# A new word order in the last triangle stage, y turned by VectorE for the last batch, and put-off pieces at fixed groups

## The chip, the cores and the metric

The kernel runs on one core of one Trainium2 chip. The metric is the device time of one execution in microseconds. A core has five engines that run their own instruction lists in order: TensorE (PE, with its weight loads PEld), VectorE (DVE), ScalarE (ACT), GpSimd (POOL) and SyncE (SP), which here issues nearly all DMAs. They wait for each other through semaphores.

## The reference, cut to what matters

Two layers on `x` of shape (4, 64, 64, 256), all in float32. The first is self-attention over the 4096 positions of each batch element, with a residual; the second takes its result, here called y, as a 64 x 64 grid of pairs and does "triangle" attention with 8 heads, then a layer norm, an MLP and another layer norm.

```python
# layer 0, per batch element, hw = 4096 positions
f, g, v = xt @ Wf + bf, xt @ Wg + bg, xt @ Wh + bh
beta = softmax(g @ f.T)                 # 4096 x 4096
y = x + (beta @ v) @ Wo + bo
# layer 1, N = 64, 8 heads of 32
q, k, v1, v2 = y @ Wq, y @ Wk, y @ Wv1, y @ Wv2
scores = einsum('bilhd,bljhd->biljh', q, k) / sqrt(32)
att = softmax(scores, axis=2)           # over l
out = einsum('biljh,bilhd,bljhd->bijhd', att, v1, v2)
h = layer_norm(y + out.reshape(...) @ Wo)
h = relu(h @ W1 + b1) @ W2 + b2 + h
return layer_norm(h)
```

## The kernel before, in words

The four batch elements ("batches" 0 to 3) go one after the other. Each has a first-layer stage and a triangle stage; what is left of batch 3 after its triangle runs in a closing loop. The program order is written out by hand: nothing reorders the instructions of an engine inside `run`. The last few lines of the kernel (1633 and on) stand outside of that, and the framework puts them where it finds room.

**First-layer stage (`layer0`).** It has 8 blocks of 512 queries, and each block has 8 groups g (k = g mod 8) of 512 keys. In a group TensorE makes scores (L552) and the weighted values (L579), ScalarE the exponentials e (L564), two buffers of them, and VectorE adds e into esum (L586; L584 in group 0). In group 7 VectorE folds esum and splits it into the tile `part` (L589 to L596). The finished block is worked off in the groups of the next block, by the list `parts`: in group 0 the denominator den on TensorE (L604), its reciprocal (L608) and two bounds (L618) on VectorE; in group 1 y itself (L631, L632) and its store; in groups 2 to 7 the projections q, k, v1, v2 (L646, L678), each copied by ScalarE to a staging tile of three (`st`) and stored by SyncE.

For b > 1 the groups also carry the *put-off pieces* of batch b - 2: 16 pieces of 256 tokens, each loaded back (`recall`), added to its residue and measured (`settle`, VectorE, L1073 to L1137), then `rooted` (ScalarE), `polished` (VectorE, L1175 to L1178), `scaled` (ScalarE, L1197) and `finish`ed (GpSimd, L1287 and L1288, and the store of the output at L1289). A piece starts in every third group: line 761 gives the groups after its start at which each step comes.

**Triangle stage (`next_layer1`, `step_words`).** 32 steps. A step has 8 products R0 to R7 of the turned weights and v2 (L1007); VectorE makes the first five of an even step and the first six of an odd one, GpSimd the others, into three and two buffers. Each product is accumulated by TensorE (A0 to A7, L1017) into two PSUM tiles, which ScalarE copies out (T0, T1, L1027). Further words: S sums (L932), W weights (L942), t turns them on TensorE (L959), c copies a part for GpSimd (L967), V the stationary operand (L986), sp/e scores of a later head pair and their exponentials (L905, L915). In between run the words of the pieces of the batch before: h heads (L1120 and the transposes that add y, L1125), sa statistics, fa affine, ht turning (L1220), hT and hU its copies (L1225), m and r the MLP's first half (L1253, L1262), z its second (L1273, L1279), so sums (L1151, L1155), rr roots, pp polish (on GpSimd, L1181 to L1192), fo affine and fi finish (GpSimd).

One *period* holds two steps (0 and 1 of each word's first digit) and one piece. `ORDER_LAST` lists the words of a period for batch 3. `A14/2` means accumulate product 4 of the odd step of the period two before; "/1" the period before; "/-1" the next. There are 12 periods with scores, and 16 pairs of steps in all. Batch 3's triangle finishes all pieces of batch 2 and begins pieces 0 and 1 of batch 3.

PSUM tiles come from three pools of two: scores and accumulators ("a"), pieces ("b": hp, htp, mp, zp), turned weights and others ("c"). A buffer is taken from those that were freed.

**Heads.** A piece's heads are Wo times the attention output plus y. y lies in memory with channels first, so TensorE turns it on its way into the sum, two transposes per half piece:

```python
            for cc in range(2):
                nc.tensor.matmul(
                    hp[:, n, ts(cc, P)], yc[:, cc, ts(n, P)], ident, start=False, stop=(cc == 1),
                    is_transpose=True,
                )
```

**Closing loop (`alone`).** 15 turns and an end, for the pieces of batch 3. In a turn TensorE does the heads of piece t+2, the turning of t+1, the second MLP half of t and the first of t+1; VectorE does the statistics of t+2 (`stats_a`), their polish, the residue of t+1 (L1244, L1245), the finish of t-1 (L1287, L1288), the addition and statistics of t (L1145, `stats_o`) and their polish, in this order; ScalarE makes the roots, affines, copies and `rectify`.

**Limits.** All sums and bounds of all batches are kept in `dens`; at the end two reductions over it (L1635, L1636) decide if a safe version must run (it does not).

Of the kernel before, what the change touches and what calls it, by code (L numbers as in the profile page):

```python
# [10 lines left out]
F32 = mybir.dt.float32  # L11
# [39 lines left out]
ORDER_LAST = """  # L51
    r0/1 A10/2 A11/2 m1/1 R14/2 R05/1 S1/1 R15/2 T10/2 sp/1 A14/2 A16/2 r1/1 e0/1 e1/1 A15/2 A05/1 T11/2 R04/1
    A04/1 z0/1 W1/1 R03/1 V1/1 fi/2 S0 z1/1 t1/1 so/1 R06/1 R00/1 c1/1 sa A03/1 R07/1 R02/1 A06/1 A02/1 A00/1
    rr/1 pp/1 W0 R01/1 A07/1 A01/1 fo/1 fa T01/1 R12/1 t0 T00/1 R17/1 h1/-1 sf/1 R13/1 h0/-1 f0/1 ht f1/1 R16/1
    hU A13/1 hT A12/1 A17/1 R11/1 c0 R10/1 m0 V0
""".split()
# [18 lines left out]
def attention_then_triangle_kernel(  # L75
# [130 lines left out]

    dens = ctile([P, NB, 256 + 16], "dens")

# [237 lines left out]
    class Late:  # L446
# [5 lines left out]
        def load(self, q):  # L452
            self.y = []
            for cc, tag in enumerate(("A", "yc")):
                t = work.tile([P, 512], F32, tag=tag, name="yb", bufs=1)
# [42 lines left out]
    def layer0(b, F, safe, rest, ahead):  # L498
# [7 lines left out]
        io["v2"] = dram.tile([N, C, N], F32, tag="v2", name="v2d")  # L506
        io["v1"] = dram.tile([T, C], F32, tag="v1", name="v1d")
        L = Layer1(b, io, safe)

# [104 lines left out]
        def bounds(qb):  # L614
            for j, (t, op) in enumerate(ends.pop(qb)):
                if not safe:
                    c0 = 256 + 2 * qb + j
                    nc.vector.tensor_reduce(dens[:, b, c0 : c0 + 1], t, AX.X, op)  # L618

# [6 lines left out]
        def output(qb):  # L626
            col = ts(qb, QB)
            o = oT.pop(qb)
            for cc in range(2):
                y_ps = pb("y")  # L630
                nc.tensor.matmul(y_ps, wo0_sb[:, 0, ts(cc, P)], o, start=True, stop=True)  # L631
                nc.vector.scalar_tensor_tensor(  # L632
                    y(qb, cc), y_ps, bo_sb[:, cc : cc + 1], yT[cc][:, col], ALU.add, ALU.add
                )
                nc.sync.dma_start(out=io["y"][ts(cc, P), col], in_=y(qb, cc))


# [90 lines left out]
        if late:  # L728
            parts[3] = [lambda qb: proj(qb, "k", 0)]
            parts[4] = [lambda qb: proj(qb, "v2", 0)]  # L730
            parts[5] = [proj1_half]
            parts[6] = [lambda qb: proj(qb, "q", 1)]
            parts[7] = [lambda qb: proj(qb, "k", 1)]
        last = NQB - 1
        for r in range(4):
            score(0, r)
        for g in range(8 * NQB):
# [112 lines left out]
    class Layer1:  # L850
        def __init__(self, b, io, safe):
            self.b, self.io, self.safe = b, io, safe

            self.aT = dram.tile([C, 2, N // 2, N], F32, tag="aT", name="aT")
            io["a"] = self.aT
            self.S, self.v2, self.qk, self.v1, self.att, self.ao = {}, {}, {}, {}, {}, {}
            self.R, self.begun, self.acc, self.rec, self.e = {}, {}, {}, {}, {}


# [61 lines left out]
        def sums(self, step):  # L921
# [8 lines left out]
            else:  # L930
                den = dens[:, self.b, ts(step, IG)]
            nc.vector.tensor_reduce(den, rows, AX.X, ALU.add)  # L932
# [109 lines left out]


    class Tokens:
        def __init__(self):
            self.ios = []
            self.A, self.htp = {}, {}
            self.h, self.hT, self.hT2, self.hid, self.z, self.zp, self.hps = {}, {}, {}, {}, {}, {}, {}
# [46 lines left out]
        def load(self, tt, far=False):  # L1095
# [4 lines left out]
            if far:  # L1100

                tag = ("v2", "S", "qk")[t % 3]
                both = big.tile([P, 2, 2, 256], F32, tag=tag, name="A", bufs=4 if tag == "v2" else 2)
                A, yc = both[:, 0].rearrange("p c (i j) -> p c i j", j=N), both[:, 1]
            else:
                A = work.tile([P, 2, 4, N], F32, tag="A", name="A", bufs=1)
                yc = work.tile([P, 2, 256], F32, tag="yc", name="yc", bufs=1)
# [3 lines left out]
            nc.sync.dma_start(out=yc, in_=io["y"][:, ts(t, 256)].rearrange("(c p) t -> p c t", p=P))  # L1111
            self.A[tt] = A, yc

        def heads(self, tt, n, psum=pb, new=None):
            if n == 0 if new is None else new:
                self.hps[tt] = psum("hp").rearrange("p (n c) -> p n c", n=2)
            hp = self.hps[tt]
            A, yc = self.A[tt]
            for cc in range(2):
                nc.tensor.matmul(  # L1120
                    hp[:, n, :], A[:, cc, ts(n, 2), :].rearrange("p i j -> p (i j)"), wo1_sb[:, cc, :],
                    start=(cc == 0), stop=False,
                )
            for cc in range(2):
                nc.tensor.matmul(  # L1125
                    hp[:, n, ts(cc, P)], yc[:, cc, ts(n, P)], ident, start=False, stop=(cc == 1),
                    is_transpose=True,
                )

# [8 lines left out]

        def stats_a(self, tt):
            self.stats(self.hps[tt], 0)  # L1140

# [292 lines left out]
    def first_layer1(L, ahead, F):  # L1434
# [56 lines left out]
    def next_layer1(b, L, rest, ahead, F):  # L1491
# [32 lines left out]
        def of_piece(word, q):  # L1524
# [9 lines left out]
            elif word == "sa" and first:  # L1534
                moments(q - 1)
                if own:
                    rest.stats(rest.hps[tt], 0)
# [53 lines left out]
        mps[1] = {}  # L1591
        for period in range(NP + 4):
            for word, late in words_of(ORDER_LAST if own else ORDER):
# [85 lines left out]
```

## Time and profile before

| | us |
|---|---|
| median of 3 runs | 3628.52 (3628.36 to 3633.21) |
| profiled execution | 3633.17 |
| its span, first to last instruction | 3631.40 |
| last triangle stage, from GpSimd's first product | from 3025.36 |
| first heads of the closing loop | 3472.68 |

| engine | busy us | share of the span |
|---|---|---|
| TensorE | 3522.3 | 97% |
| VectorE | 2823.5 | 78% |
| ScalarE | 1923.8 | 53% |
| GpSimd | 1779.2 | 49% |

How to read it: the span is the traced execution; the execution's own time is 1.8 us longer, and this execution was 4.65 us above the median. The ends of matmuls are modelled, so TensorE's busy time covers short gaps; the distance from one start to the next is what a word costs. A line with a bracket at its end tells how long the engine was idle before the instruction and what ended that. The mean granted TensorE clock of the profile is 0.994 of full speed.

### The profile page before, as it was taken

To read this page: it belongs to the slowest core of one execution; us is meant where nothing else is said; L and a number is where in the kernel's file an instruction comes from. 1 tells how busy PE (TensorE), PEld (TensorE's weight loads), DVE (VectorE), ACT (ScalarE), POOL (GpSimd) and SP (SyncE) were. 2 spreads that over 40 slices of the span, in tenths; PEclk is the share of its full clock that TensorE was granted. 3 is DMA by queue.
4 is the path that set the end of the run, shared out by engine and by line. 5 is a ranking of instruction groups with operands and counts; after the bars stand their busy time and mean duration, and the time that the engine had idled before them with its cause. 6 is when DMAs were issued, how large, how long until landed. Compare 5 with 4: busy or idle time off the path is not lost.

```text
span 3631.4 us, 58644 instructions
## 1 busy us (share of the span) xinstructions
PE 3522.3 (97%) x22282; PEld 1895.3 (52%) x22282; DVE 2823.5 (78%) x2558; ACT 1923.8 (53%) x4221; POOL 1779.2 (49%) x904
## 2 busy tenths in 40 slices
PE   9999999988999999999999999999899999999998
PEld 6555444434555555554455555554455555555477
DVE  4777499996555569999777549999877756999976
ACT  3444455544444366665444446666444436777655
POOL 5000099995000068889211018889611106999920
PEclk9999999999999999999999999999999999999999
DMA  9544555455111354425423254343622235441221
GB/s 174 135 131 127 136 151 137 122 134 136 47 52 52 82 145 108 101 68 107 110 91 95 67 146 109 89 104 76 132 87 95 80 93 134 92 96 46 68 68 55
DMA packets 492594, 370.15 MB, mean 102 GB/s; under 512 B 303184, under 2 KB 434000, under 8 KB 483472
## 3 DMA queue, kind: packets, MB, share of 16 engines
q1 hardware_dynamic: 443264, 339.36, 34.8%
q0 software_dynamic: 36160, 19.94, 5.3%
q10 hardware_dynamic: 12880, 7.01, 0.7%
q8 instruction: 178, 2.92, 0.4%
q14 instruction: 112, 0.92, 0.1%
HBM read 205.73 MB, written 160.43 MB: 101 GB/s over the span
## 4 chain that ended last, share of the span: by engine, by line
PE 67%; POOL 8%; DVE 6%; issue 4%; ACT 1%; DMA 1%; SPq 0%; ACTq 0%; POOLq 0%; DVEq 0%
PE o L579 16%; PE acc L1017 16%; POOL Rp L1007 7%; PE proj L646 6%; PE mp L1253 5%; PE zp L1273 5%; PE s L552 4%; PE sp L905 3%; PE hp L1120 3%; DVE R L1007 2%; PE v1p L678 2%; PE att L959 1%; PE y L631 1%; DVE rec L608 1%; PE htp L1220 1%
## 5 line engine op out<-in xcount | busy, mean ns | idle before, releaser
L1007 POOL TENSOR_TENSOR Rp<-attP,v 128x2048 f32<-128x2048 f32 x328 | 1491.4, 4579 | 409.7 <-ACT attP L967 367.0
L1007 DVE TENSOR_TENSOR R<-att,v 128x2048 f32<-128x2048 f32 x696 | 1546.1, 2279 | 68.6 <-PE acc L1017 49.9
L579 PE MATMUL o<-e,v 128*128 128x512 f32 x2048 | 1043.9, 593 | 0.0
L586 DVE TENSOR_TENSOR esum<-esum,e 128x2048 f32<-128x2048 f32 x224 | 518.8, 2316 | 398.4 <-ACT e L564 395.9
L564 ACT ACTIVATE e<-s 128x1024 f32<-128x1024 f32 x512 | 522.3, 1023 | 529.2 <-PE s L552 438.7
L552 PE MATMUL s<-gT,fT 128*128 128x512 f32 x1024 | 786.7, 770 | 8.7 <-ACT e L564 4.7
L1017 PE MATMUL acc<-R,wsel 128*32 128x512 f32 x5568 | 702.8, 599 | 26.5 <-DVE R L1007 19.6
L579 PEld LDWEIGHTS o<-e,v 128*128 128x128 f32 x2048 | 388.2, 190 | 276.8 <-issue 234.0
L1027 ACT COPY ao<-acc 128x1024 f32<-128x1024 f32 x256 | 256.4, 1013 | 290.4 <-PE acc L1017 205.8
L1017 PE MATMUL acc<-Rp,wsel 128*32 128x512 f32 x2624 | 344.3, 596 | 25.6 <-POOL Rp L1007 23.2
L1017 PEld LDWEIGHTS acc<-R,wsel 128*32 128x32 f32 x5568 | 155.5, 109 | 393.7 <-issue 273.9
L552 PEld LDWEIGHTS s<-gT,fT 128*128 128x128 f32 x1024 | 194.5, 190 | 244.7 <-issue 230.8
L1287 POOL TENSOR_TENSOR hz<-hz,log_bc 128x512 f32<-128x512 f32 x32 | 47.1, 1471 | 542.8 <-ACT hz L1197 474.4
L1181 POOL TENSOR_SCALAR nt<-mv 128x2 f32<-128x2 f32 (+1 forms) x49 | 9.4, 192 | 565.2 <-DVE mv L1137 560.1
L942 ACT ACTIVATE es<-S,rd 128x64 f32<-128x64 f32 x1024 | 258.3, 338 | 15.0 <-DVE rd L934 13.1
L1253 PE MATMUL mp<-hT,w 128*128 128x256 f32 x1024 | 244.4, 384 | 1.7 <-ACT hT L1225 1.7
L1273 PE MATMUL zp<-w,hid 128*128 128x256 f32 x1024 | 239.4, 384 | 0.8 <-ACT hid L1262 0.8
L1253 PEld LDWEIGHTS mp<-hT,w 128*128 128x128 f32 x1024 | 186.5, 190 | 53.0 <-ACT attP L967 12.6
L1273 PEld LDWEIGHTS zp<-w,hid 128*128 128x128 f32 x1024 | 188.0, 190 | 47.8 <-issue 14.7
L608 DVE RECIPROCAL rec<-den 128x512 f32<-128x512 f32 x32 | 107.4, 3357 | 109.7 <-PE den L604 104.4
L1017 PEld LDWEIGHTS acc<-Rp,wsel 128*32 128x32 f32 x2624 | 80.7, 110 | 214.1 <-issue 144.9
L915 ACT ACTIVATE S<-sp 128x512 f32<-128x512 f32 x128 | 131.6, 1094 | 78.0 <-PE sp L905 78.0
(192 smaller groups left out, 3688.4 us busy)
## 6 DMA issues: line engine op xcount, KB each, us to landing
v<-v2d SPq DMA_DIRECT2D x44, 512.0 KB
v1c<-v1d SPq DMA_DIRECT2D x128, 128.0 KB
aT<-ao SPq DMA_DIRECT2D x1024, 16.0 KB
A<-aT SPq DMA_DIRECT2D x256, 64.0 KB
hz<-raw SPq DMA_DIRECT2D x32, 512.0 KB
y<-yT SPq DMA_DIRECT2D x56, 256.0 KB
q<-st SPq DMA_DIRECT2D x56, 256.0 KB
k<-st SPq DMA_DIRECT2D x52, 256.0 KB
```

Of the source, the lines that this page charges most:

```text
L552: nc.tensor.matmul(s_ps[r // 2][:, r % 2, :], fT[tt][:, ts(r * 4 + n, P)], gT[qb // 4][:, ts(qb % 4, QB)], start=True, stop=not safe,)
L564: nc.scalar.activation(e[g][:, 2 * j : 2 * j + 2, :], s_ps[j], AF.Exp)
L579: nc.tensor.matmul(o_ps[qb], F.v[tt][:, r * 4 + n, :], es[:, r, :], start=(k == 0 and r == 0), stop=(k == 7 and r == 3),)
L586: nc.vector.tensor_tensor(esum[qb], esum[qb], es, ALU.add)
L608: nc.vector.reciprocal(rec, den)
L646: nc.tensor.matmul(ps, w[:, cc, rows], y(qb, cc), start=(cc == 0), stop=(cc == 1))
L942: nc.scalar.mul(e[:, i, :], rows[:, i, :], rec[:, i : i + 1])
L1007: eng.tensor_tensor(R, src.unsqueeze(1).to_broadcast([P, D, N]), v2[h], ALU.mult)
L1017: nc.tensor.matmul(acc[32 * c : 32 * c + 32, n % 2, :], w[:, n, c, 16 * h : 16 * h + 32], R[:, ts(c, 8), :].rearrange("p d j -> p (d j)"), ...
L1027: nc.scalar.copy(self.ao[step][:, ts(np, 2)].rearrange("p k d j -> p k (d j)"), self.acc[step][np])
L1253: nc.tensor.matmul(self.mp[:, fc % 2, :], w1_sb[:, cc, ts(fc, P)], self.hT[tt][:, cc, :], start=(cc == 0), stop=(cc == 1),)
L1273: nc.tensor.matmul(zp[:, n, :], self.hid[tt][:, fc, ts(n, P)], w2_sb[:, fc, :], start=(fc == 0), stop=(fc == 3 and tt not in self.hT2),)
```

## The change

Five edits:

1. `ORDER_LAST` has its words in another order, and some of them with another period. The rule that moved two words of the first period (A05, A04) is dropped.
2. For batch 3 (`turned_ahead`), y is also kept with tokens first, in a new buffer `yt`. VectorE turns it block by block in 32 x 32 squares (`turn_y`): blocks 0 to 6 in group 5 of the next block, with the tile in the buffer that `part` uses ("hid"); the last after its bounds, with its stores put off to the start of period 1 of the triangle (`L.owed`). Each block goes out in four stores in runs of 256 bytes.
3. The heads of batch 3 have no transposes. Before the statistics VectorE adds the loaded rows of `yt` to the heads in PSUM (`add_y`).
4. The put-off pieces have fixed places in a block: three pieces in blocks 0 and 1, two in 2 to 6, none in 7, with the settles in groups 2, 3 and (third piece) 5.
5. `dens` holds one batch; each batch's limits are reduced in group 1 of the next batch's first layer, the last batch's at the end.

```diff
-    r0/1 A10/2 A11/2 m1/1 R14/2 R05/1 S1/1 R15/2 T10/2 sp/1 A14/2 A16/2 r1/1 e0/1 e1/1 A15/2 A05/1 T11/2 R04/1
-    A04/1 z0/1 W1/1 R03/1 V1/1 fi/2 S0 z1/1 t1/1 so/1 R06/1 R00/1 c1/1 sa A03/1 R07/1 R02/1 A06/1 A02/1 A00/1
-    rr/1 pp/1 W0 R01/1 A07/1 A01/1 fo/1 fa T01/1 R12/1 t0 T00/1 R17/1 h1/-1 sf/1 R13/1 h0/-1 f0/1 ht f1/1 R16/1
-    hU A13/1 hT A12/1 A17/1 R11/1 c0 R10/1 m0 V0
+    A07/2 sf/2 T01/2 f0/2 R16/2 sp/1 f1/2 A10/2 R17/2 fa/1 fo/2 A12/2 R15/2 S1/1 ht/1 h1 e1/1 fi/2 h0 hU/1 hT/1
+    e0/1 t0/1 R13/2 m0/1 r0/1 A13/2 R14/2 A14/2 R11/2 A15/2 c0/1 A16/2 V0/1 W1/1 A17/2 A11/2 R00/1 V1/1 R01/1
+    m1/1 t1/1 R05/1 S0 T11/2 T10/2 r1/1 A00/1 W0 R03/1 A01/1 R06/1 A05/1 c1/1 R02/1 z1/1 R04/1 z0/1 A02/1 so/1
+    A03/1 R07/1 sa rr/1 R10/1 R12/1 T00/1 A06/1 pp/1 A04/1
...
-    dens = ctile([P, NB, 256 + 16], "dens")
+    dens = ctile([P, 256 + 16], "dens")
+    lims = ctile([P, 2, NB], "lims")
+    def limits(b):
+        for j, op in enumerate((ALU.min, ALU.max)):
+            nc.vector.tensor_reduce(lims[:, j, b : b + 1], dens, AX.X, op)
...
+        def turn_y(qb, **where):
+            t = work.tile([P, 16, 2, 32], F32, name="yr", **where)
+            for cc in range(2):
+                rows = y(qb, cc).rearrange("p (k t) -> p k t", t=32)
+                for k in range(4):
+                    nc.vector.transpose(t[:, ts(k, 4), cc, :], rows[:, ts(k, 4), :])
+            def kept():
+                for r in range(4):
+                    nc.sync.dma_start(
+                        out=io["yt"][ts(qb, QB), ts(r, 64)].rearrange("(k t) c -> t k c", t=32),
+                        in_=t[ts(r, 32)].rearrange("t k h c -> t k (h c)"),
+                    )
+            return kept
...
+        if turned_ahead(b):
+            parts[5].append(lambda qb: turn_y(qb, tag="hid", bufs=1)())
...
-                for do, late in ((rest.finish, 7), (rest.scaled, 6), (rest.polished, 5), (rest.rooted, 4), (rest.settle, 3), (rest.recall, 0)):
-                    if (g - late) % 3 == 0 and 0 <= g - late < 3 * NP:
-                        do(NP * (b - 2) + (g - late) // 3)
+                first = 3 * qb if qb < 2 else 2 + 2 * qb
+                for t in range(3 if qb < 2 else 2 if qb < last else 0):
+                    for do, at in (
+                        (rest.recall, t), (rest.settle, 2 + t + t // 2), (rest.rooted, 3 + t + t // 2),
+                        (rest.polished, 4 + t + t // 2), (rest.scaled, 5 + t + t // 2), (rest.finish, 7),
+                    ):
+                        if k == min(at, 7):
+                            do(NP * (b - 2) + first + t)
+            if g == 1 and b > 0 and not safe:
+                limits(b - 1)
...
         bounds(last)
+        if turned_ahead(b):
+            L.owed = turn_y(last, tag="k8")
...
+            src = io["yt"][ts(t, 256)] if turned_ahead(b) else io["y"][:, ts(t, 256)]
+            nc.sync.dma_start(out=yt, in_=src.rearrange("(n p) c -> p n c", p=P))
...
-                    start=(cc == 0), stop=False,
-                )
-            for cc in range(2):
-                nc.tensor.matmul(
-                    hp[:, n, ts(cc, P)], yc[:, cc, ts(n, P)], ident, start=False, stop=(cc == 1),
-                    is_transpose=True,
-                )
+                    start=(cc == 0), stop=(cc == 1 and turned_ahead(tt // NP)),
+                )
+            if not turned_ahead(tt // NP):
+                for cc in range(2):
+                    nc.tensor.matmul(
+                        hp[:, n, ts(cc, P)], self.yt[tt][:, cc, ts(n, P)], ident, start=False, stop=(cc == 1),
+                        is_transpose=True,
+                    )
+
+        def add_y(self, tt):
+            hp, yt = self.hps[tt], self.yt.pop(tt)
+            if not turned_ahead(tt // NP):
+                return
+            for n in range(2):
+                own = hp[:, n, :].rearrange("p (h r c) -> p h r c", h=2, r=4)
+                nc.vector.tensor_tensor(own, own, yt[:, n, :].rearrange("p (r h c) -> p h r c", h=2, r=4), ALU.add)
...
         def stats_a(self, tt):
+            self.add_y(tt)
             self.stats(self.hps[tt], 0)
...
         for period in range(NP + 4):
+            if period == 1:
+                L.owed()
             for word, late in words_of(ORDER_LAST if own else ORDER):
                 i = period - late
-                if own and i == 0 and word in ("A05", "A04"):
-                    for m in (4, 5) if word == "A04" else ():
-                        step_word("A", 0, m)
-                elif word[0] in "RATSWVtc":
+                if word[0] in "RATSWVtc":
...
-    flat = dens.rearrange("p b n -> p (b n)")
-    nc.vector.tensor_reduce(lim[:, 0:1], flat, AX.X, ALU.min)
-    nc.vector.tensor_reduce(lim[:, 1:2], flat, AX.X, ALU.max)
+    limits(NB - 1)
+    nc.vector.tensor_reduce(lim[:, 0:1], lims[:, 0], AX.X, ALU.min)
+    nc.vector.tensor_reduce(lim[:, 1:2], lims[:, 1], AX.X, ALU.max)
```

More of the change, by code (lines that the diff above doesn't have):

```diff
@@ L453, in load @@
             self.y = []
-            for cc, tag in enumerate(("A", "yc")):
-                t = work.tile([P, 512], F32, tag=tag, name="yb", bufs=1)
+            for cc, tag, bufs in ((0, "A", 1), (1, "yc", 1)):
+                t = work.tile([P, 512], F32, tag=tag, name="yb", bufs=bufs)
                 nc.sync.dma_start(out=t, in_=self.io["y"][ts(cc, P), ts(q, 512)])
@@ L507, in layer0 @@
         io["v1"] = dram.tile([T, C], F32, tag="v1", name="v1d")
+        io["yt"] = dram.tile([T, C], F32, tag="yt", name="yt")
         L = Layer1(b, io, safe)
@@ L617, in bounds @@
                     c0 = 256 + 2 * qb + j
-                    nc.vector.tensor_reduce(dens[:, b, c0 : c0 + 1], t, AX.X, op)
+                    nc.vector.tensor_reduce(dens[:, c0 : c0 + 1], t, AX.X, op)
         def y(qb, cc):
@@ L857, in __init__ @@
             self.R, self.begun, self.acc, self.rec, self.e = {}, {}, {}, {}, {}
+            self.owed = lambda: None
         def fetch_qk(self, pair, first=False):
@@ L930, in sums @@
             else:
-                den = dens[:, self.b, ts(step, IG)]
+                den = dens[:, ts(step, IG)]
             nc.vector.tensor_reduce(den, rows, AX.X, ALU.add)
@@ L1039, in store, with turned_ahead @@
                 )
+    def turned_ahead(b):
+        return b == NB - 1
     class Tokens:
@@ L1046, in __init__ @@
             self.ios = []
-            self.A, self.htp = {}, {}
+            self.A, self.yt, self.htp = {}, {}, {}
             self.h, self.hT, self.hT2, self.hid, self.z, self.zp, self.hps = {}, {}, {}, {}, {}, {}, {}
@@ L1103, in load @@
                 both = big.tile([P, 2, 2, 256], F32, tag=tag, name="A", bufs=4 if tag == "v2" else 2)
-                A, yc = both[:, 0].rearrange("p c (i j) -> p c i j", j=N), both[:, 1]
+                A, yt = both[:, 0].rearrange("p c (i j) -> p c i j", j=N), both[:, 1]
             else:
                 A = work.tile([P, 2, 4, N], F32, tag="A", name="A", bufs=1)
-                yc = work.tile([P, 2, 256], F32, tag="yc", name="yc", bufs=1)
+                yt = work.tile([P, 2, 256], F32, tag="yc", name="yt", bufs=1)
             for c in range(2):
@@ L1110, in load @@
                     nc.sync.dma_start(out=A[:, c, o : 4 : 2, :], in_=io["a"][ts(c, P), o, ts(t, 2), :])
-            nc.sync.dma_start(out=yc, in_=io["y"][:, ts(t, 256)].rearrange("(c p) t -> p c t", p=P))
-            self.A[tt] = A, yc
+            src = io["yt"][ts(t, 256)] if turned_ahead(b) else io["y"][:, ts(t, 256)]
+            nc.sync.dma_start(out=yt, in_=src.rearrange("(n p) c -> p n c", p=P))
+            self.A[tt], self.yt[tt] = A, yt
         def heads(self, tt, n, psum=pb, new=None):
@@ L1117, in heads @@
             hp = self.hps[tt]
-            A, yc = self.A[tt]
+            A = self.A[tt]
             for cc in range(2):
@@ L1535, in of_piece @@
                 moments(q - 1)
+                rest.add_y(tt)
                 if own:
@@ L1592, in next_layer1 @@
         for period in range(NP + 4):
+            if period == 1:
+                L.owed()
             for word, late in words_of(ORDER_LAST if own else ORDER):
                 i = period - late
-                if own and i == 0 and word in ("A05", "A04"):
-                    for m in (4, 5) if word == "A04" else ():
-                        step_word("A", 0, m)
-                elif word[0] in "RATSWVtc":
+                if word[0] in "RATSWVtc":
                     step_word(word[0], 2 * i + int(word[1]), int(word[-1]))
```

## The prediction

> **What bounds the kernel now.** I read the busy shares on the page first:
>
> ```profile
> PE 3522.3 (97%) x22282; PEld 1895.3 (52%) x22282; DVE 2823.5 (78%) x2558; ACT 1923.8 (53%) x4221; POOL 1779.2 (49%) x904
> ```
>
> TensorE is busy nearly always, so a gain is either TensorE work taken away or one of its few waits. Next the busy time in chosen windows (columns: window, length, then busy time of PE, PEld, DVE, ACT, POOL, granted clock, DMA share, GB/s): one period of the last triangle stage, one of its end, and the closing loop.
>
> ```profile
> 3113.53:3141.30 27.77, 27.77 (x257) 14.96 (x260) 26.87 (x20) 19.68 (x54) 26.65 (x15) 1.00 0.57 128
> 3390.00:3417.00 27.00, 26.11 (x192) 13.09 (x188) 26.79 (x20) 17.60 (x52) 26.35 (x15) 1.00 0.23 55
> 3500.00:3550.00 50.00, 50.00 (x253) 44.06 (x252) 35.78 (x111) 26.31 (x70) 0.00 (x0) 1.00 0.30 83
> ```
>
> A triangle period is 27.76 us of TensorE, with VectorE and GpSimd within 1.2 us of it: a new order of words can gain little there and can lose by any wait. The last four periods have no scores and turn at 27.2 us (GpSimd's triples of products start at 3375.86, 3403.07, 3430.28): there GpSimd binds. The closing loop is TensorE alone.
>
> Last the timelines. VectorE's reciprocal marks each block of 512 queries in batch 3's first layer, and TensorE's own list shows its waits:
>
> ```profile
> 2689.17 3.36 DVE L608 RECIPROCAL rec<-den 128x512 f32<-128x512 f32 x1 [2.42 <-PE den L604]
> 2740.00 3.36 DVE L608 RECIPROCAL rec<-den 128x512 f32<-128x512 f32 x1 [5.00 <-PE den L604]
> 2792.04 3.36 DVE L608 RECIPROCAL rec<-den 128x512 f32<-128x512 f32 x1 [3.62 <-PE den L604]
> ```
> ```profile
> 2751.43 1.98 PE L646 MATMUL proj<-yT,wq 128*128 128x512 f32 x4 [0.93 <-DVE yT L632]
> ```
>
> Blocks take 50.83 us, but 52.04 where that wait stands. The same list has it at 2905.12, and in batch 2 at 1888.69 and 2042.35: four blocks.
>
> **The put-off pieces.** Today a piece starts every third group. A settle (L1073 to L1137, 3.4 us of VectorE) lands in group 0 of a block when the group number divides by 24, behind the reciprocal. It delays the sum of group 1 and the addition that makes y (L632), and the projection waits. The new groups put settles at 2, 3 and 5 only, so I take 4 x 1.2 = **-4.8 us**. What is late next: in group 0 nothing, since VectorE waited 5.0 us for den when no settle stood in group 7. The first two blocks now hold three pieces: group 5 gets a sum 2.3, a settle 3.4 and, in batch 3, the turning 8 x 0.39 = 3.1 (L356), 8.8 us against some 7.9 of TensorE, but the exponentials that reuse the sum's buffer come two groups later: I count about 4.7 us of cover from the lists of one block. SyncE's finish stores now wait at group 7 for GpSimd (1.47 + 1.73 per piece), with the next recall and the y stores behind them, which nobody reads for 6 us. Bounds: -4.8 if all hold, 0 if as many blocks collide elsewhere.
>
> **The turning of y.** Seven turnings stand in groups 5; the eighth falls after the last bounds, where VectorE idles 20.8 us (the wait before L932). Each makes four stores of 512 runs of 256 bytes, issued by SyncE at 0.47 each (the stores at L359). The tile shares its buffer with `part`, so L594 in group 7 waits until they land. Queue 1 took 34.8% of 16 engines' 3631 us for 443264 packets, 46 ns each; 2048 packets are 5.8 us. First issue is some 7 us before L594 (2724.2 against 2680.36 + 50.83), and den has 5.6 us more: cost 0, at most 1 us per microsecond beyond that, in 7 blocks. The Trainium skill speaks against such stores (DMA: Bandwidth & Descriptors, Specifications): below 512 bytes a transfer misses line rate and is done by read-modify-write. If that doubles the packet's time, my estimate by that page is 11.7 us, which still ends before den waits; the trace's under-512 packets aren't timed apart.
>
> `L.owed` sends the last four stores at the start of period 1: 1.9 us of SyncE, before the loads of that period, bounds 0 to +2, taken 0.
>
> **The heads of batch 3.** In the closing loop one turn is:
>
> ```profile
> 3521.96 1.03 PE L1120 MATMUL hp<-wo,A 128*128 128x256 f32 x4
> 3522.82 0.38 PE L1125 MATMUL hp<-ident,A 128*128 128x128 f32 x2
> 3523.04 1.03 PE L1120 MATMUL hp<-wo,A 128*128 128x256 f32 x4
> 3523.90 0.38 PE L1125 MATMUL hp<-ident,A 128*128 128x128 f32 x2
> 3524.12 0.60 PE L1220 MATMUL htp<-ident,h 128*128 128x128 f32 x4
> ```
> ```profile
> 3522.40 0.16 DVE L1175 SCALAR_TENSOR_TENSOR nt<-mv,rs 128x2 f32<-128x2 f32 x1 [0.60 <-ACT rs L1165]
> ...
> 3524.32 0.43 DVE L1136 BATCH_NORM_STATS2 st<-hp 128x6 f32<-128x256 f32 x1 [1.18 <-PE hp L1125]
> ...
> 3526.10 0.16 DVE L1175 SCALAR_TENSOR_TENSOR nt<-mv,rs 128x2 f32<-128x2 f32 x1 [0.60 <-ACT rs L1165]
> ```
>
> Each pair of transposes holds TensorE 0.22 us (start to start), so a turn loses 0.44: 9.51 becomes 9.07. But the additions come ahead of the statistics on VectorE, which waits 1.18 for the heads and twice 0.60 for ScalarE's roots. The last two are in its chain and stay. So its turn is 9.51 - 1.18 = 8.33, and two additions come to it. The trace has no addition from PSUM back into PSUM; the nearest is:
>
> ```profile
> L1343 DVE TENSOR_TENSOR z<-zp,z 128x256 f32<-128x256 f32 x2 | 0.8, 404 | 0.0
> ```
>
> With dispatch 0.42 each, VectorE needs 9.17 and takes TensorE's place as the bound. Gain 0.34 a turn, 13 turns (14 with heads, the first bound otherwise): **-4.4 us**. Bounds: additions hidden, 14 x 0.44 = -6.1; additions as dear as the 512-column one at L1145 (0.684 + 0.03 each), 8.33 + 1.42 = 9.75, 13 x 0.24 = +3.1. I take the row of equal size. The two heads of batch 3 inside the triangle save 0.9 us of TensorE where GpSimd binds: 0.
>
> The Trainium skill says to turn 128x128 on TensorE where the result may lie in PSUM (VectorE: DVE Perf Modes, Rules for kernel authors), which is the old form. Its 390 ns for such a turn would make TensorE's part 1.56 us a turn; here it is 0.44, and since VectorE's 9.17 binds, the gain would still be 4.4.
>
> **The new order.** Costs of the words, from starts in the period at 3113: A 0.86, leaving a run of A for another shape about 0.13, entering one 0.1; sp 1.91, z 3.9, the h pair 2.16, ht and t 0.43, m 1.73. Both orders have four runs of A: the old 5, 6, 3, 2 with m1 beside sp; the new 5 (A02 A03 A06 A04 A07), 2, 6, 3, with sp between two runs, one change of shape fewer: 27.55 instead of 27.76. Then VectorE. A product takes the buffer freed earliest: R03 starts at 3114.60, 1.14 after A14 (3113.46), though A04 too is ahead of it in the program. So in the new order R11 waits for A13 (A15 comes after it). From R11 to R14 stand 11 products at 2.21, two sums at 0.84, statistics 1.16: 27.2. A14 follows 0.15 later, A13 stands 0.86 earlier: 1.14 + 27.2 + 0.15 - 0.86 = 27.65, slightly above TensorE. GpSimd: 5 x 4.54 + 1.85 + 2.65 = 27.2. ScalarE's T11 must free a bank for A00; after V1, which waits for A11, it ends about 0.3 us in time. So 27.65 against 27.76 in 11 periods: -1.2. The last four stay at 27.2: 0. The filling: TensorE waits 1.0 of 28.0 us in 3030 to 3058 now, and in the new order t1 waits for the first weights about as long: 0, bounds -2 and +2. Bounds of the stage: all engines already near their sums, -6; an unseen wait of 0.7 a period, +9.
>
> **The limits.** Two reductions of 1088 columns (L1635, L1636, 1.27 each), among the last products, become two of 272: by slope from L932 (512 columns, 0.67) some 0.42 each, and two of 4 columns, 0.14 each. 1.4 us of VectorE where its last products end the stage: **-1.0**. The other three batches' pairs fall into a group of idle VectorE: 0.
>
> **Sum.** -4.8 - 4.4 - 1.2 - 1.0 = -11.4. The profiled execution took 3633.2 us (span 3631.4 and 1.8 around it), giving 3621.8; the median of the runs is 4.65 below it, giving 3628.5 - 11.4 = **3617**.
>
> **Rivals.** (a) *The end of the chain only changes hands*: additions at 0.59 or more leave the closing turn at 9.51 and the order gives nothing; the put-off pieces and the limits alone remain, 3623. For it: the PSUM write is unseen. Chance 0.26. (b) *Slower: R11 waits for A15.* If the three product buffers went strictly in turn, R11 would need R15's, and the loop R14, A14, A15, R11 gives 1.14 + 27.2 + 0.15 + 0.86 = 29.35: +1.6 in 11 periods, +2.15 in four, +26 instead of -1.2, so 3645. It decides from some 1.3 us a period on. For it: three buffers, each product three takes after its forerunner. Against: hp keeps one of two banks over four takes of the other now, which a strict turn could not do. With other waits of that size, chance 0.11. (c) *The stores don't do what they should*: they land later than L594's cover and each of 7 blocks pays; at 1 us each, 3624, inside (a)'s chance.
>
> **Numbers.** Forecast 0.63, (a) 0.26, (b) 0.11. 0.2% is 7.3 us, about what a measurement of this kernel can tell from no change; faster means below 3621.3. The forecast counts as faster, (a) and (c) as the same, (b) as slower. Range: best cases of the closing loop, blocks and order together (-6.1, -4.8, -6, -1) reach 3611, with some filling 3609; on the other side the neutral cases with a mild wait in the order reach 3630. Only (b) and little else is left out.
>
> **What would show it.** Blocks of 50.83 us throughout the first layer of batches 2 and 3, no wait for yT at L646; turns of about 9.2 us with VectorE's wait for hp gone; triangle periods of 27.6. Wrong would be: a wait before R11 and then A11 each period; additions above 0.5 us; L594 waiting for a DMA.

## The result and the profile after

The changed kernel takes 3636.31 us in the median of 12 runs (3630.75 to 3644.45), the kernel before 3632.99 in 12 runs beside them (3624.61 to 3635.48). The ratio is 1.0016, its 95% interval 1.0009 to 1.0024: a little slower, where 3617 was predicted. The prediction built on three runs of the kernel before with a median of 3628.52; against the twelve, 4.5 of the 19.3 us that it missed by are this base, and the change itself was forecast at -11.4 and came at +3.3.

The span of the profiled execution went from 3631.4 to 3639.3. The changed kernel's profiled execution lies 4.8 us above the median of its runs (3641.14), that of the kernel before 0.2. Its twelve runs go with the mean granted clock that each shows (3630.75 at 0.995, 3644.45 at 0.991), so differences between the two traces below add up to more than that of the medians.

I read the blocks of the first layer first. The list of VectorE's reciprocals (L615 now) for batch 3:

```profile
2649.38 3.35 DVE L615 RECIPROCAL rec<-den 128x512 f32<-128x512 f32 x1
2703.12 3.36 DVE L615 RECIPROCAL rec<-den 128x512 f32<-128x512 f32 x1 [2.96 <-PE den L611]
2753.94 3.36 DVE L615 RECIPROCAL rec<-den 128x512 f32<-128x512 f32 x1 [3.62 <-PE den L611]
```

From the second line on the distance is 50.82: the blocks of 52.04 are gone, as predicted. But the first distance is 53.74, and the first reciprocal has no bracket at all: VectorE didn't wait for den, it came late itself.

TensorE's list for the end of block 0 and the start of block 1 in batch 2 shows what that costs, and the windows over the same place show the clock (columns: window, length, busy time of PE, PEld, DVE, ACT, POOL, granted clock, DMA share, GB/s):

```profile
1774.78 0.50 PE L559 MATMUL s<-gT,fT 128*128 128x512 f32 x1 [2.13 <-ACT e L571]
...
1780.25 0.49 PE L611 MATMUL den<-part,ones_f 128*128 128x512 f32 x1 [0.62 <-DVE part L603]
...
1782.94 0.50 PE L559 MATMUL s<-gT,fT 128*128 128x512 f32 x1 [2.20 <-ACT e L571]
...
1784.39 1.91 PE L586 MATMUL o<-e,v 128*128 128x512 f32 x2
```
```profile
1774.00:1780.00 6.00, 4.85 (x13) 2.37 (x13) 5.90 (x5) 1.65 (x2) 0.73 (x1) 1.00 0.12 44
1780.00:1784.00 4.00, 1.55 (x5) 0.86 (x5) 3.90 (x7) 2.91 (x4) 1.86 (x2) 1.00 0.00 0
1784.00:1788.00 4.00, 4.00 (x8) 1.88 (x7) 3.96 (x5) 1.02 (x1) 0.68 (x1) 0.57 0.57 179
```

Scores wait for exponentials; those wait for their buffer, which VectorE hasn't summed yet. The three brackets are 4.95 us in the ten up to 1782.94; after them the granted clock is at 0.50 from 1784.32 to 1787.73, 3.41 us (0.57 is the mean of the window shown), so the pair of `o` took 1.91 instead of the 1.02 of its neighbours. My estimate is some 1.7 us more (3.41 x 0.5). Batch 3 shows the same, with the clock at 0.50 from 2651.30 to 2654.71.

Now a triangle period, one of the end and the closing loop, as they were shown before:

```profile
3177.55:3205.11 27.56, 27.56 (x256) 14.99 (x252) 26.79 (x19) 19.80 (x56) 26.61 (x15) 1.00 0.19 49
3403.00:3430.00 27.00, 26.17 (x190) 13.21 (x189) 26.79 (x20) 17.99 (x53) 26.35 (x15) 1.00 0.34 85
3510.00:3560.00 50.00, 50.00 (x242) 43.38 (x241) 40.97 (x123) 26.90 (x72) 0.00 (x0) 1.00 0.31 85
```

The period is 27.56 instead of 27.77. In the closing loop VectorE is now busy 40.97 of 50 us instead of 35.78. One turn of it:

```profile
3549.33 1.89 PE L1160 MATMUL hp<-wo,A 128*128 128x256 f32 x8
...
3551.09 0.16 DVE L1225 SCALAR_TENSOR_TENSOR nt<-mv,rs 128x2 f32<-128x2 f32 x1 [0.60 <-ACT rs L1215]
...
3551.75 0.90 DVE L1177 TENSOR_TENSOR hp<-hp,A 128x256 f32<-128x256 f32 x2
...
3552.69 0.43 DVE L1185 BATCH_NORM_STATS2 st<-hp 128x6 f32<-128x256 f32 x1
...
3558.52 1.89 PE L1160 MATMUL hp<-wo,A 128*128 128x256 f32 x8
```

The heads have no transposes, the statistics no longer wait for hp, the wait of 0.60 for the roots remains (the other, at 3554.47, too), and the turn is 9.19. The four turns after the first two of the loop took 9.07, the rest 9.19.

The two traces, stage by stage (us; differences of starts):

| | before | after | difference |
|---|---|---|---|
| start to batch 1's last reciprocal | 1264.27 | 1265.03 | +0.76 |
| batch 1's last to batch 2's last reciprocal | 862.66 | 868.69 | +6.03 |
| the same, batch 2 to 3 | 862.78 | 867.47 | +4.69 |
| batch 3's last reciprocal to GpSimd's first product | 35.65 | 35.66 | 0 |
| that to the closing loop's first heads | 447.32 | 446.80 | -0.52 |
| first to last heads of the closing loop | 125.37 | 120.83 | -4.54 |
| last heads to the end | 33.3 | 34.8 | +1.5 |

The sum is the span's +7.9. The loss sits in two rows, those of the put-off pieces. In them the first block (first scores to its reciprocal) grew from 44.21 to 49.83 and 48.06, and block 1 from 50.81 and 50.83 to 53.74; of these 2.9 us in block 1 some 1.7 are the clock.

### The profile page after: what moved, and what is told of

Same layout as the page of the kernel before. It is cut to its first block, busy times and chain, and to the rows that moved or that the text cites. A ratio compares the mean times of both kernels' runs of the same rounds, so it can differ in the third digit from the quotient of the medians.

```text
span 3639.3 us, 58664 instructions
## 1 busy us (share of the span) xinstructions
PE 3518.2 (97%) x22218; PEld 1888.9 (52%) x22218; DVE 2861.2 (79%) x2662; ACT 1925.5 (53%) x4221; POOL 1770.9 (49%) x904
## 4 chain that ended last, share of the span: by engine, by line
PE 63%; DVE 10%; POOL 6%; issue 4%; DMA 2%; ACT 2%; SPq 1%; ACTq 0%; DVEq 0%; POOLq 0%
PE acc L1052 16%; PE o L586 16%; PE proj L669 6%; POOL Rp L1042 5%; DVE R L1042 5%; PE s L559 4%; PE mp L1303 4%; PE zp L1323 4%; PE sp L940 3%; PE v1p L701 2%; PE hp L1160 2%; PE y L638 1%; PE att L994 1%; DVE esum L593 1%; DVE st L1185 1%
## 5 line engine op out<-in xcount | busy, mean ns | idle before, releaser
L615 DVE RECIPROCAL rec<-den 128x512 f32<-128x512 f32 x32 | 107.4, 3357 | 104.9 <-PE den L611 99.5
```

## The experiments

**Theory:** block 0 of a batch has no projections, so its groups are short (4.36 us of TensorE instead of about 6.35, 50.82 / 8); three settles don't fit beside VectorE's sums there. **Rivals:** three pieces are too many for any block; the first settle stands on its load; y's turning costs the time. In the tables "block 0" is first scores to reciprocal, "blocks 1-7" first to last reciprocal, for batches 2 / 3. Each run has its own runs of the kernel before beside it.

### Old places of the pieces

```diff
-                first = 3 * qb if qb < 2 else 2 + 2 * qb
-                for t in range(3 if qb < 2 else 2 if qb < last else 0):
...
+                for do, late in ((rest.finish, 7), (rest.scaled, 6), (rest.polished, 5), (rest.rooted, 4), (rest.settle, 3), (rest.recall, 0)):
+                    if (g - late) % 3 == 0 and 0 <= g - late < 3 * NP:
+                        do(NP * (b - 2) + (g - late) // 3)
```

> The changed kernel with the put-off pieces back at every third group, as before; the new order, the turned y and the per-batch limits stay. Theory (the short groups of the first block, which has no projections, cannot hold three settles): all that was lost goes away, the four collisions of 1.2 us come back, and what remains is the closing loop (4.54 shorter in its turns, 1.47 longer at its end) and 0.5 of the triangle stage: about 3.5 us under the kernel before, ratio 0.999, first layers of the third and fourth batch at 862.7 each between the last reciprocals. Rival (the turned y's transposes, stores or sums cost the first layer its time): the fourth batch stays near 867, ratio 1.000 or above.

Measured: 3627.54, ratio 0.9990 (0.9981 to 0.9999); first layers 862.90 and 862.80. The loss goes, the collisions are back. The other four edits together are worth 4.7 us by the medians.

### Only the new places

The kernel before with edit 4 alone (the reverse of the lines above).

> The kernel before with nothing but the new places of the put-off pieces (3, 3, 2, 2, 2, 2, 2 at fixed groups): y turned by TensorE and the old order stay. Theory (three settles in the first block fill VectorE before that block's folds, whatever else was changed): the third and the fourth batch's first layer take 867 to 869 between the last reciprocals instead of 862.7, the rest stays, and the time is 10 to 11 over the kernel before: ratio 1.003. Rival (the loss needs y's transposes or the limits beside them): 862 or less in both, ratio 0.999.

Measured: 3642.09, ratio 1.0028 (1.0017 to 1.0040); first layers 868.96 and 867.54, as in the changed kernel. The places alone make the loss; y's turning has no part in it.

### No piece in the first block

```diff
-                first = 3 * qb if qb < 2 else 2 + 2 * qb
-                for t in range(3 if qb < 2 else 2 if qb < last else 0):
+                per = (0, 3, 3, 3, 3, 2, 2, 0)
+                first = sum(per[:qb])
+                for t in range(per[qb]):
```

> The changed kernel with the sixteen pieces shared out as 0, 3, 3, 3, 3, 2, 2 over the first seven blocks: none in the first block, three in the next four, the same groups within a block. Theory (short groups of the first block): every block from the second on takes 50.8 us and the first 43.0, so the first layers come to 860.3 each, and the time is about 8.4 under the kernel before, ratio 0.9977. Rival (three pieces are too many for any block, since finish, polish and settles slow VectorE): the second to fifth block take 53 to 54 each, 2.2 to 2.9 more in eight blocks, some 18 to 23 us on top: ratio 1.003 or more.

Measured: 3622.51, ratio 0.9971 (0.9960 to 0.9981); first layers 860.10 and 860.16. The start of batch 2's list:

```profile
1773.77 3.36 DVE L615 RECIPROCAL rec<-den 128x512 f32<-128x512 f32 x1 [2.22 <-PE den L611]
1824.59 3.36 DVE L615 RECIPROCAL rec<-den 128x512 f32<-128x512 f32 x1 [2.98 <-PE den L611]
```

Every block is 50.82, those with three pieces too, and VectorE waits for den in each. This rules out that three pieces are too many for any block. VectorE in 8 us slices of block 0 (same columns), first this kernel, then the changed one:

```profile
1754.00:1762.00 8.00, 8.00 (x24) 4.17 (x22) 3.89 (x3) 3.50 (x4) 0.00 (x0) 1.00 0.00 0
1762.00:1770.00 8.00, 8.00 (x23) 4.14 (x23) 5.84 (x6) 3.69 (x4) 0.00 (x0) 1.00 0.00 0
```
```profile
1756.00:1764.00 8.00, 6.55 (x18) 2.97 (x17) 7.72 (x14) 3.84 (x6) 0.00 (x0) 1.00 0.00 0
1764.00:1772.00 8.00, 8.00 (x23) 4.16 (x22) 7.72 (x13) 4.99 (x9) 4.92 (x4) 1.00 0.09 33
1772.00:1780.00 8.00, 5.50 (x15) 2.37 (x13) 7.79 (x6) 1.94 (x3) 2.73 (x1) 1.00 0.09 33
```

With nothing put off, VectorE (the third busy number) is busy 3.89 and 5.84 of 8; with three settles it is full for 24 us on end, up to the folds that close the block, and TensorE (the first) has holes.

### Two or three pieces in the first block, settled in four ways

```diff
+                per = (2, 3, 3, 2, 2, 2, 2, 0)
...
+                    at0 = (4, 5)[t] if qb == 0 else 2 + t + t // 2
-                        (rest.recall, t), (rest.settle, 2 + t + t // 2), (rest.rooted, 3 + t + t // 2),
-                        (rest.polished, 4 + t + t // 2), (rest.scaled, 5 + t + t // 2), (rest.finish, 7),
+                        (rest.recall, t), (rest.settle, at0), (rest.rooted, at0 + 1),
+                        (rest.polished, at0 + 2), (rest.scaled, at0 + 3), (rest.finish, 7),
```

The first of the four has only the line `per`: two pieces at the changed kernel's own groups, 2 and 3. The next two move these settles to (4, 5), as shown, and to (2, 5). The fourth has three pieces, `per = (3, 3, 2, 2, 2, 2, 2, 0)`, settled in (3, 5, 6).

> The changed kernel with the sixteen pieces shared out as 2, 3, 3, 2, 2, 2, 2: two in the first block, settled in its groups 2 and 3. Theory (three settles are too many for the short groups): two fit, as two did before, the first block takes 43 to 44, and the time is 6 to 8.4 under the kernel before, ratio 0.998. Rival (a settle two groups after its recall stands on its load, whatever their number): VectorE still idles some 3 to 4 us at the first settle, the first block takes 45 or more in both batches, and no more than 4 us are won against the kernel before: ratio 0.999 to 1.000.

> As the run with 2, 3, 3, 2, 2, 2, 2 pieces, but the two of the first block are recalled in groups 0 and 1 as there and settled in groups 4 and 5 instead of 2 and 3. What that run lost in the first block against an empty one (3.2 us in the third batch, 1.9 in the fourth) has two candidates. If it was the stand on the load (VectorE idle 4.1 us at the first settle), the loads have landed by group 4 and the first block goes back to some 44.2, as with the old places. If it was two settles in neighbouring groups (3.3 each and 0.8 of polish, against 2.07 that a group of 4.36 leaves beside a 2.29 sum), it stays near 45.5 or above, with exponentials waiting for sums.

> The same with settles in groups 2 and 5: the first stands on its load as in the run before, the two are three groups apart as in the old places. If the stand on the load is what costs, the first block stays at 45.3 to 46.6; if neighbouring settles cost, it goes back to 44.2 or less although VectorE still idles at the first settle.

> Three pieces in the first block (3, 3, 2, 2, 2, 2, 2), settled in groups 3, 5 and 6 instead of 2, 3 and 5 of the changed kernel, so that the first has a group more for its load. If the number is what costs (three settles with their polishes take 12.3 us, six groups' worth of the 2.07 that VectorE has over), the first block still takes 46.5 or more and the second block carries part of it on. If load and neighbourhood were all, it comes down to 45 or less.

| settles of block 0 in groups | time | ratio (95%) | block 0 | blocks 1-7 |
|---|---|---|---|---|
| none | 3622.51 | 0.9971 (0.9960 to 0.9981) | 43.40 / 43.43 | 348.90 / 348.90 |
| 2, 5 | 3624.94 | 0.9981 (0.9971 to 0.9990) | 43.84 / 43.40 | 349.82 / 349.60 |
| 2, 3 | 3627.53 | 0.9987 (0.9978 to 0.9996) | 46.56 / 45.31 | 348.94 / 348.94 |
| 4, 5 | 3628.57 | 0.9988 (0.9979 to 0.9997) | 44.49 / 44.50 | 350.14 / 351.83 |
| 2, 3, 5 (changed kernel) | 3636.31 | 1.0016 (1.0009 to 1.0024) | 49.83 / 48.06 | 351.81 / 351.81 |
| 3, 5, 6 | 3641.31 | 1.0031 (1.0020 to 1.0042) | 49.72 / 49.72 | 351.60 / 352.54 |

My theory, "two fit", fell in its simple form: at 2 and 3 two pieces lose 3.2 and 1.9 against none. So did the load as the cause: at 2 and 5 VectorE still stands at the first settle,

```profile
1751.42 0.69 DVE L1114 TENSOR_TENSOR hz<-hz,lag_bc 128x512 f32<-128x512 f32 x1 [3.99 <-DMA hz<-raw]
```

and loses 1.4 and 0.7 in all. As I read the lists, what orders the rows is how much lag VectorE has when it must sum; no run changes that lag alone. A short group leaves it 4.36 - 2.29 = 2.07 beside a sum; a settle with its polish takes 4.1, so two groups. Neighbours (2, 3 or 4, 5) owe more than the buffers cover; near the block's end the debt meets the folds, the reciprocal and the next block's first sum. With the last settle in group 6 the polish stands ahead of that sum and waits for ScalarE's roots, GpSimd's sweeps stretch it (0.16 becomes 0.90 and 1.11), and TensorE stands idle for 6 us; in that stand its clock falls to 0.50 at 1776.82 and stays there for 6.83 us:

```profile
1776.12 0.90 DVE L1227 SCALAR_TENSOR_TENSOR nt<-mv,rs 128x2 f32<-128x2 f32 x1 [1.58 <-ACT rs L1217]
...
1777.26 1.11 DVE L1229 SCALAR_TENSOR_TENSOR rn<-nt,rs 128x2 f32<-128x2 f32 x1
...
1778.48 1.22 DVE L591 COPY esum<-e 128x2048 f32<-128x2048 f32 x1
```
```profile
1780.65 0.80 PE L559 MATMUL s<-gT,fT 128*128 128x512 f32 x1 [6.21 <-ACT e L571]
```
```profile
1777.00:1780.65 3.65, 0.00 (x1) 0.01 (x1) 3.55 (x6) 2.06 (x4) 2.16 (x3) 0.50 0.20 72
```

The third settle is the dear one: from (2, 3) to (2, 3, 5) is 6.1 and 5.6 us a batch. The pair at 4 and 5 costs batch 3 1.7 us more than batch 2 in block 1, and the traces show the clock there: in batch 3 it is at 0.50 from 2642.07 to 2645.48, at the start of block 1, in batch 2 it stays at 1.00 (3.41 x 0.5 is 1.7). The other rows carry the clock too: it falls at the seam of block 0 and 1 in both batches with (2, 3, 5) and with (3, 5, 6), and in neither with none, (2, 5) or (2, 3).

### y turned by VectorE, old places, old order

Both edits go back; the turned y and the limits stay.

> The kernel before with y turned by VectorE for the last batch and the limits batch by batch, and nothing else: old places of the put-off pieces, old order of the triangle stage. Theory: the closing loop gives its 3.1 (4.54 in the turns less 1.47 at the end), the first layers stay at 862.7: ratio 0.9992. Against the kernel with the new order and old places it tells what the order is worth: the theory has 0.5 us, the prediction had 1.2. Rival (the transposes and stores of y cost time in the fourth batch's first layer, hidden so far under what the pieces lose there): its first layer takes 863.5 or more and the ratio is 1.000.

Measured: 3627.31, ratio 0.9985 (0.9976 to 0.9994). First layers 863.04 and 863.02, 0.2 to 0.4 above the kernel before in both batches, though batch 2 has no turning: it costs nothing there. The closing loop takes 120.93 from first to last heads, as after.

### The order alone

The kernel before with the new `ORDER_LAST` and without the rule for A05 and A04.

> The kernel before with nothing but the new order of the last triangle stage's words. Theory, from the kernels with and without it (both with y turned by VectorE): the last product's matmuls come 2.2 us earlier, the last piece's second half follows them, and the closing loop starts only some 0.3 to 0.5 us earlier: ratio 1.000. The prediction had 1.2 us, ratio 0.9997; the interval of the time cannot tell these apart, the stretch from GpSimd's first product to the first heads of the closing loop in the trace can: 446.8 to 447.0 against 446.1 (447.32 before).

Measured: 3632.03, ratio 1.0001 (0.9992 to 1.0010). The stage took 446.08: the prediction's number (446.1), not the 446.8 to 447.0 of my theory. GpSimd's polish comes once a period, so its starts measure the periods. The filling in GpSimd's list:

```profile
3037.50 0.20 POOL L1181 TENSOR_SCALAR nt<-mv 128x4 f32<-128x4 f32 x1
3069.07 0.20 POOL L1181 TENSOR_SCALAR nt<-mv 128x4 f32<-128x4 f32 x1
3096.65 0.19 POOL L1181 TENSOR_SCALAR nt<-mv 128x4 f32<-128x4 f32 x1
```

| interval between polishes | before | y turned only | order only | after |
|---|---|---|---|---|
| second (filling) | 30.10 | 30.11 | 31.57 | 33.15 |
| third to twelfth, each | 27.77 | 27.76 | 27.57 | 27.57 |
| last four, each | 27.21 | 27.23 | 27.24 | 27.24 |

The order wins 0.2 in ten periods, 2.0 us, and gives 1.5 of it back in the filling; with the turned y another 1.6 goes there. Another 0.8 is won behind the last polish (16.24 us to the closing loop's first heads instead of 17.05), where nothing was counted. The windows (same columns) show the place in the filling, first of the order alone, then of the changed kernel, both around the second run of scores:

```profile
3039.83:3043.83 4.00, 2.88 (x102) 2.64 (x98) 4.00 (x3) 3.10 (x5) 4.00 (x1) 1.00 0.93 160
3043.83:3047.83 4.00, 4.00 (x61) 2.31 (x51) 2.23 (x3) 2.96 (x7) 4.00 (x2) 1.00 0.11 21
```
```profile
3052.85:3056.85 4.00, 2.75 (x98) 2.51 (x93) 4.00 (x3) 3.10 (x5) 4.00 (x1) 1.00 1.19 221
3056.85:3060.85 4.00, 4.00 (x58) 1.53 (x48) 1.23 (x3) 2.41 (x5) 4.00 (x2) 0.58 0.36 77
```

The new order puts the scores of the first period (`sf`) and of the second (`sp`) next to each other, and the second wait for the loads of k, 1.12 us with the order alone, 1.25 after. How much of the 1.5 is this wait no run separates: the kernel before has waits of 0.54 and 0.46 in its own filling. In the changed kernel the clock is then at 0.50 for 3.41 us from 3057.49 (0.58 over the window), which by the same estimate is 1.7 us, about the other 1.6; with the order alone it stays at 1.00.

### Stores of y later, GpSimd in the closing loop

Both start from the kernel with no piece in the first block; the second has both edits.

```diff
                 if tt > t0:
-                    self.finish(tt - 1, V)
+                    self.finish(tt - 1)
...
-            if period == 1:
+            if period == 3:
                 L.owed()
```

> The kernel with no piece in the first block (0, 3, 3, 3, 3, 2, 2), and in the closing loop the two gains and shifts of a piece before the last are done by GpSimd, idle there, instead of VectorE, which loses 1.38 us of work a turn. Theory (the turns of 9.19 and the 1.5 more at the end are VectorE's lateness): all turns take 9.07, 1.0 less over eight, and the end after the last heads loses up to 1.5: 1 to 2.5 us under the kernel it starts from, ratio 0.9966. Rival (GpSimd's sweeps stretch VectorE's at the same time, as the 2.29 sums went to 2.8 beside them in the first block): two sweeps of 1.3 to 3.3 us stretch what runs beside them by 1 us or more a turn, the turns go to 9.5 or above and the time 3 or more above it.

Measured: 3621.56, ratio 0.9972 (0.9961 to 0.9982): the time can't tell it from its forerunner. The trace can: all turns take 9.07 (120.00 from first to last heads instead of 120.84), and the end is 34.1 instead of 34.6, so about 1.35 won. Both theories hold something: VectorE loses two sweeps of 0.69 a turn, but its polish beside GpSimd is stretched,

```profile
3515.09 1.27 POOL L1339 TENSOR_TENSOR z<-z,lob_bc 128x512 f32<-128x512 f32 x1
3515.26 1.12 DVE L1228 SCALAR_TENSOR_TENSOR rn<-nt,rs 128x2 f32<-128x2 f32 x1
```

and its busy time falls by 0.1 a turn only. The rival's turns of 9.5 didn't come, and of the 1.5 at the end about 0.8 stays.

> The kernel with no piece in the first block and the closing loop's gains and shifts on GpSimd, and besides the four stores of the last block's turned y issued at the head of period 3 of the last triangle stage instead of period 1. Theory: in period 1 the scores wait 1.25 us for the loads of k that stand behind and beside those stores, TensorE works little for 2 us, and the clock granted to it falls to 0.5 to 0.7 for 4 us right after; with the order alone the same wait is 1.12 and the clock stays at 1.00. With the stores away from there the wait is at most 1.12, the clock stays at 1.00, the second interval between GpSimd's polishes goes from 33.3 to 31.6, and the stage is 1.5 us shorter: ratio 0.9968 against the kernel before. Rival (the slow clock comes from the new order itself, or the longer fill from VectorE's sums of y): the interval stays at 33, the clock falls again, ratio 0.9972.

Measured: 3621.38, ratio 0.9974 (0.9964 to 0.9984). The rival held: the wait for k is 1.15, the clock falls, the second interval is 33.30.

```profile
3037.10:3041.10 4.00, 4.00 (x56) 1.41 (x46) 1.70 (x3) 2.53 (x5) 4.00 (x2) 0.69 0.10 21
```

So the stores aren't the cause, and neither is the length of the wait: the clock falls to 0.50 there in all nine kernels that have both the new order and the turned y, after waits of 0.87 to 1.33, and not in the order alone after 1.12. What decides is not shown, but the traces narrow it. Within a trace the stretches at 0.50 start whole multiples of 3.413 us apart (in the changed kernel 1784.32, 2651.30 and 3057.49: 254 and 119 times) and, but for the last one at the end of the kernel, last 3.41, 6.83 or 10.24 us. In the nine kernels 0.75 us or more of the wait lies in the one 3.41 us stretch of this raster before the fall, and TensorE has 0.5 us or less of matmuls other than the small scores in it. With the order alone a boundary (3042.35) cuts the wait into 0.61 and 0.51, and the two stretches hold 0.7 and 1.0 us of other matmuls. So where the raster falls can tell the ten apart without the turned y; that is one trace each, and no run tests it.

The three kernels with no piece in the first block are the fastest here, some 10 us under the kernel before and 14 under the changed one; among them the time doesn't decide.

## Why the prediction was wrong, step by step

**The put-off pieces: wrong, and this alone is most of the error.** -4.8 was forecast, +10.7 came (6.03 + 4.69). The mechanism named was there: the four blocks of 52.04 are 50.82 and the waits for yT are gone, 4.85 us. The step that failed is "The first two blocks now hold three pieces: group 5 ... 8.8 us against some 7.9 of TensorE ... I count about 4.7 us of cover from the lists of one block." That block was one with projections. There the count holds (three pieces cost nothing in blocks 1 to 4 of the run without a piece in block 0). Block 0 has none: it takes 43.4 instead of 50.8, a group leaves VectorE 2.07 us, and the pieces lost 15.5 us (10.7 and the 4.85 saved elsewhere) in it and at its seam to block 1. The bound "0 if as many blocks collide elsewhere" was no bound, since it priced a collision at the 1.2 seen where TensorE had other work to do.

**The closing loop: right in its turns, its end left out.** -4.4 was forecast, -4.54 measured from first to last heads. The addition took 0.42 to 0.43 as taken from the row of equal size (0.47 from start to start), and after four turns at TensorE's 9.07 VectorE became the bound at 9.19, against 9.17. What failed is that the step stopped at the last turn with heads: in the one after it TensorE waits for `hid` 1.54 where it waited 0.23 (first the kernel before, then the changed one), and last heads to end grew by 1.5.

```profile
3608.39 3.72 PE L1273 MATMUL zp<-w,hid 128*128 128x256 f32 x16 [0.23 <-ACT hid L1262]
3615.81 3.72 PE L1323 MATMUL zp<-w,hid 128*128 128x256 f32 x16 [1.54 <-ACT hid L1312]
```

Net -3.0. The size is loose: the end took 34.5 to 35.0 in the eight traces with the turned y and VectorE's finish, and 33.3, 33.6 and 33.8 in the three without. With GpSimd's help the turns went to 9.07 and half of this came back; the other half isn't explained by a run.

**The order: right in sum by luck.** 27.65 a period was forecast, 27.57 came; VectorE's rule (the buffer freed earliest) held. The filling, taken as 0 with bounds of 2, cost 1.5 alone and 3.1 with the turned y, and the 0.8 behind the last polish were not in the sum. Alone the order gave -1.24 in the trace, where -1.2 was forecast; in the changed kernel the stage gave -0.52, the limits included.

**Turning y, `L.owed`:** 0 was taken, 0 was measured for both; no wait stands at `part`, and the later stores changed nothing. A transpose took 0.27, not 0.39. **Limits:** eight reductions of 0.43; their -1.0 was not measured by itself. With the old order, the limits and the turned y together left the stage at 446.81 instead of 447.32; how the 0.5 is shared no run shows.

**The rivals.** (a) needed additions of 0.59: fell. (b) R11 behind A15 would have given periods of 29.35: fell. (c) fell. The forecast lacked the case that happened, a place where the pieces' new neighbours have no cover; it was named only as a bound.

## What to carry to other kernels

Cover is counted in the shortest stage that a moved piece of work can fall into, not in the stage whose list lies open: here a group of a batch's first block left VectorE 2.07 us, half of what the blocks that were read leave (6.35 - 2.29). An engine that gets several extra pieces must have paid its debt before the next thing that all wait for, so spread them and leave the last groups of a block free. When a loop gets shorter by a change of bound, count its last turns by themselves.

## What the runs showed of the hardware

A stand of TensorE can cost more than its length: after 5 us of stand in 10 the granted clock was at 0.50 for 3.41 us, and in the stand of 6.21 it fell to 0.50 some 2.4 us after its start and stayed there for 6.83. Beside the small score matmuls (32x64) it fell to 0.50 for 3.41 us after a stand of only 0.87 to 1.33, in nine kernels of ten. The falls lie on a raster of 3.413 us.

GpSimd's sweeps stretch VectorE's instructions beside them, by about 1 us whether short or long: 0.16 became 1.12 or 1.22, 0.69 became 1.77, a pair of sums took 5.53 instead of 4.5. In the closing loop with GpSimd's finish, ten of VectorE's polish instructions took 1.12 beside such a sweep, and none took more than 0.17 with no sweep beside it. An addition from PSUM into the same PSUM (128x256 float32) takes VectorE 0.42 to 0.43, some 0.02 more than the two that write elsewhere (0.39 and 0.42).
